# Second-pass products as four 32-column tiles, and a planner that counts mode changes: a four-block graph network on one core

## The chip, the core and the metric

The kernel runs on one core of a Trainium2 chip. The metric is device time in microseconds (us) of one execution. Before the change three executions took 1333.88, 1335.44 and 1337.19 us; the median is 1335.44 us. The profiled execution, from which all durations below come, has a span of 1335.1 us.

## What is computed

The input is `x` of shape (32, 512, 128) and a symmetric 0/1 adjacency `adj` of shape (32, 512, 512), both float32. Four residual blocks follow each other; each begins with a layer norm over the last axis and a ReLU:

```
h = relu(layernorm(x))
x = x + attention(h, adj)      # layer 0: q, k, v = relu(h W + b); softmax over the neighbours of q k^T; times v
h = relu(layernorm(x))
x = x + gcn_lstm(h, adj)       # layer 1: an LSTM of 128 steps over a convolution of the last 128 rows,
                               #          sigmoid((A_norm h) lstm_out)
h = relu(layernorm(x))
x = x + four_layers(h, adj)    # layer 2: four graph layers with skip inputs of width 128, 128, 256, 384
h = relu(layernorm(x))
x = x + prelu(adj (h W) + b)   # layer 3
```

The LSTM of layer 1 couples nothing across the 32 batch elements, but its 128 steps are one chain: each needs the state of the step before.

## The kernel before the change

The function `symmetric` does the work when `adj` is symmetric. (A slower general branch is entered only if a counter found a violation at the end.) It has four kinds of work:

- `pass_1(b)` for each of the 32 batch elements: layer norm, keys and values, attention of the last 128 rows alone, and the convolution that feeds the LSTM (tile `f_seq`).
- `lstm()`: 128 steps. A step is a product on TensorE (line 1200), tanh on ScalarE (lines 1226, 1241), three small operations on VectorE (lines 1233 to 1235), tanh (line 1243), one more product and a 32x32 transpose on VectorE (lines 1247 and 1248). The state of all 32 batch elements is only 32 columns wide, so TensorE is used in four *column tiles*: four products, each with a stationary operand of 128 rows and 32 columns, write four groups of 32 PSUM partitions. The function `products` issues these four.
- `pass_2(b)`: attention of the other 384 rows of an element. Its float32 products are `f_pq` (line 1278, one of 384 columns), `f_s` (line 1287, four of 384 columns) and `f_po` (line 1296, twelve of 129 columns), each with a stationary operand of the full 128 columns. For the elements in `EARLY` (before: 0 to 23) it also does the adjacency product of layer 1 (`f_pg`, eight matmuls of 512 columns in a rounded float32 format, line 1380 in `aggregate`) and sends the result to DRAM.
- `rest(b)`: the remainder of layers 1, 2 and 3. For elements outside `EARLY` it also does the `f_pg` product of layer 1 (line 1386).

In `EARLY`, too, `squares` on ScalarE, `relu_parts` on ScalarE and VectorE and `diagonal` on GpSimd belong to `pass_2`. Four calls of `fold` multiply weights of layer 2 together.

No order is written by hand. Every piece of work is recorded as an `Op` with a duration, a rank and its dependences, and `Plan.run` lays the pieces out in time on the engines (a list scheduler), then issues them in the order of their planned starts. On the chip the order per engine is fixed; an engine whose next instruction is not ready waits. Ranks below `URGENT` (1000) are the LSTM's steps; ranks from 20,000 are `pass_2`, from 30,000 `rest`. Pieces of the second pass and the folds are placed between the steps of the LSTM: an urgent piece's expected start holds back longer pieces (the test with 0.15 us). `LATE` (before: 2) elements have their `pass_2` put at the rank of `rest`. `T_STEP` is the planned duration of the LSTM's four tiles, `T_SWITCH` a fixed addition per step. PSUM has eight banks (the cell tag `mm`); one is spared for the LSTM as long as that runs (`spared`), and a test in `room` keeps the last free bank for work that is nearly due.

A float32 product appears in the profile as two records (two passes over the data), each with a weight load (LDWEIGHTS, engine PEld) and a matmul (MATMUL, engine PE); the LSTM's four tiles thus appear as eight of each. A rounded-float32 matmul appears as one.

Of the kernel before, what the change touches and what calls it, by code (L numbers as in the profile page):

```python
# [514 lines left out]


class Op:
    __slots__ = ("engines", "rank", "no", "deps", "cells", "waits", "ready", "end", "engine", "start", "next", "gap")


class Plan:
# [9 lines left out]
    ACROSS = {"PE": 0.2, "ACT": 0.16, "DVE": 0.18, "POOL": 0.18, "SP": 0.25}  # L531
    WITHIN = {"PE": 0.0, "ACT": 0.13, "DVE": 0.12, "POOL": 0.05, "SP": 0.0}
    SLACK = {"PE": 0.25, "ACT": 0.05, "DVE": 0.05, "POOL": 0.05, "SP": 0.05}

    def lag(self, a, b, urgent):

# [24 lines left out]
        c.real = real  # L561
        return c

    def op(self, engines, rank, reads=(), writes=(), after=(), gap=0.0):

        o = Op()
        o.engines, o.rank, o.no, o.gap = engines, rank, len(self.ops), gap
        deps = set(after)
        cells = []
        for acc, is_write in [(a, False) for a in reads] + [(a, True) for a in writes]:  # L570
            c, part = acc if isinstance(acc, tuple) else (acc, None)
            if c not in cells:
                cells.append(c)
            for key, (ws, rs) in c.parts.items():
                if part is None or key is None or key == part:
                    deps.update(ws)
                    if is_write:
                        deps.update(rs)
            mine = c.parts.setdefault(part, ([], []))
            if is_write:  # L580
                c.parts[part] = ([o], [])
            else:
                mine[1].append(o)
        deps.discard(o)
        o.deps = list(deps)
        o.cells = [c for c in cells if c.pool is not None]
        for c in o.cells:
            c.left += 1
        self.ops.append(o)
        return o  # L590

    def run(self, tc, queues):
# [63 lines left out]
        def room(o):  # L656

            at = 0.0
            need = {}
            for c in o.cells:  # L660
                if c not in seen:
                    if c.tag in self.fifo and self.fifo[c.tag][turn[c.tag] + need.get(c.tag, 0)] is not c:
                        return None
                    need[c.tag] = need.get(c.tag, 0) + 1
            for t, n in need.items():
                if len(slots[t]) < n + (t == self.banks and o.rank >= self.spared and self.left > 0):
                    return None
                if len(slots[t]) == n and t in self.kept and by_rank and o.rank > by_rank[-1].rank + 12:
                    return None
                at = max(at, sorted(slots[t])[n - 1])  # L670
            return at
# [2 lines left out]
            if not o.waits:  # L674
                put(o)
        done, order = 0, []
        by_rank = sorted((o for o in ops if o.rank >= self.URGENT), key=lambda o: -o.rank)
        while done < len(ops):
            best = None
            for e, cands in pools.items():  # L680
                first = None
                held = expected.get(e)
                for rank, no, o in cands:
                    r = room(o)
                    if r is None:
                        continue
                    if r:
                        r += self.HOP
                    s = max(free[e], o.ready[e], r)
                    if len(o.engines) > 1:  # L690
                        mine = s + o.engines[e][0]
                        if any(max(free[x], o.ready[x], r) + o.engines[x][0] < mine - 1e-9 for x in o.engines if x != e):
                            continue
                    if rank < self.URGENT:
                        held = s
                    elif held is not None and s < held < s + o.engines[e][0] - 0.15:
                        continue
                    if first is None or s < first[0] - 1e-9:
                        first = (s, o)
                        if s <= free[e] + 1e-9:  # L700
                            break
                if first is not None and (best is None or first[0] < best[0]):
                    best = (first[0], e, first[1])
            assert best is not None, f"no instruction can start, {done} of {len(ops)}"
            s, e, o = best
            for x in o.engines:
                pools[x].remove((o.rank, o.no, o))
            o.start, o.engine, o.end = s, e, s + o.engines[e][0]
            free[e] = o.end
            if o.rank < self.URGENT:  # L710
                foresee(o)
            for c in o.cells:
                if c not in seen:
                    seen.add(c)
                    slots[c.tag].remove(place(c, s) if c.tag == self.banks else min(slots[c.tag]))
                    if c.tag in self.fifo:
                        turn[c.tag] += 1
                c.left -= 1
                c.free_at = max(c.free_at, o.end)
                if c.left == 0:  # L720
                    slots[c.tag].append(c.free_at)
# [18 lines left out]
def symmetric(ctx, tc, x, adj, weights, cols, rows, lstm_b, prelu_a, out, fail):  # L740
# [16 lines left out]
    L = NT - 1  # L757
    NR = N - P
    MANY = 512 // (4 * B)
    LATE = 2  # L760
    EARLY = range(24)
    FOLDS = (4, 7, 10, 13)
    MOVED = range(2, B - 2)
    TURN = 32
    T_STEP, T_SWITCH = 0.24, 0.1
    assert D == P and N == 512

    BUFS = {"a": 2, "ar": 6, "x": 7, "xn": 5, "y": 5, "gs": 5, "inv": 4, "n0": 4, "n1": 4, "n2": 4, "n3": 4, "low": 3, "hp": 2, "dt": 2, "mm": 8, "st": 4, "mv": 4, "rs": 4, "sh": 4, "dg": 8, "dv": 4,
# [58 lines left out]

    def DMA(rank, kb, fn, r=(), w=(), **k):
        return plan.op({"SP": (max(0.45, t_dma(kb)), fn)}, rank, r, w, gap=2.0, **k)

    def turn_tiles(dst, src):

# [353 lines left out]
    def lstm():  # L1186
# [17 lines left out]
                products(z, k, W_IH, seq[:, k, :])  # L1204

        z = biased(0)
        PE(2_000, MANY * T_STEP, lambda z=z: first(z), [], [z], after=conv_ops)
        coming, c = z, None
        for t in range(T):
            R = t  # L1210
# [9 lines left out]
                    products(coming, k, W_IH, seq[:, t + MANY, :])  # L1220
            if t or coming is not None:
                ahead = 0.0 if coming is None else T_STEP
                PE(R, T_SWITCH + ahead + (T_STEP if t else 0.0), step, [], ([z] if t else []) + ([coming] if coming else []),
                   after=last, gap=-ahead)
            th = new("th", (P, 4, TURN), f"f_th_{t}")
            ACT(R, 0.22, lambda th=th, z=z, k=k: nc.scalar.activation(th.t[:, :3, :], z.t[:, k, :3, :], AF.Tanh), [z], [(th, 0)])
            cn = new("c", (P, TURN), f"f_c_{t}")
# [26 lines left out]
    def pass_2(b):  # L1254
# [29 lines left out]
        es = []  # L1284
        for j in range(NT):
            s = bank(f"f_s_{b}_{j}", (P, NR), whole=False)
            PE(R, t_mm(NR), lambda s=s, j=j: nc.tensor.matmul(s.t, keys.t[:, bass.ts(j, P)], q.t, start=True, stop=True),  # L1287
               [keys, q], [s])
            e = new(f"n{j}" if j < 3 else "y", (P, NR), f"f_e_{b}_{j}")
            ACT(R, t_act(NR), lambda s=s, e=e: nc.scalar.activation(e.t, s.t, AF.Exp), [s], [e])  # L1290
            DVE(R, t_dve(NR), lambda e=e, j=j: nc.vector.tensor_mul(e.t, e.t, rows_of(j)), [(mask, j)], [e])  # L1291
            es.append(e)
        po = bank(f"f_po_{b}", (P, L, P + 1), whole=False)
        for t in range(L):
            for j in range(NT):
                PE(R, t_mm(P), lambda t=t, j=j: nc.tensor.matmul(  # L1296
                    po.t[:, t, :], es[j].t[:, bass.ts(t, P)], v.t[:, j, :], start=(j == 0), stop=(j == NT - 1)),
                    [es[j], v], [po])
# [46 lines left out]
    def sums_of_1(rank, b, xc, ar, rs):  # L1345
# [6 lines left out]
        xp = relu_parts(rank, xs, f"c{b}")  # L1352
        pg = bank(f"f_pg_{b}")
        diagonal(rank, ar, OP.add, b in EARLY)
        first = aggregate(rank, xp, ar, pg, b in EARLY)
        gT = xc if b in EARLY else new("gs", (P, N), f"f_gT_{b}")
        evict(rank, N, lambda: gT.t if b not in EARLY else flat(gT.t), lambda: pg.t, [pg], [gT])
        return gT, first
# [15 lines left out]
            parts.t[:, :, 1, :], xs.t, 0.0, f32(parts.t[:, :, 0, :]), OP.max, OP.subtract), [xs, (parts, 0)], [(parts, 1)])  # L1374
        return parts

    def aggregate(rank, parts, ar, pg, single=False):

        for k, j in ((k, j) for k in range(2) for j in range(NT) if single):
            last = PE(rank, t_r(N), lambda k=k, j=j: nc.tensor.matmul(  # L1380
                pg.t, parts.t[:, j, k, :], ar.t[:, j, :], start=(k == 0 and j == 0), stop=(k == 1 and j == NT - 1)),
                [(parts, k), ar], [pg])
        for k in range(0 if single else 2):
            def fn(k=k):
                for j in range(NT):
                    nc.tensor.matmul(pg.t, parts.t[:, j, k, :], ar.t[:, j, :], start=(k == 0 and j == 0),  # L1386
# [277 lines left out]
```

## Time and profile before

| stage (us from the start) | what runs | length | TensorE busy | VectorE busy | ScalarE busy |
|---|---|---|---|---|---|
| 0 to 183 | first pass | 183 | 173.3 | 155.4 | 109.3 |
| 183 to 528 | the LSTM, second pass beside it | 345 | 328.9 | 286.0 | 232.8 |
| 528 to 1335 | `rest` | 807 | 786.8 | 568.3 | 490.6 |

The stages are cut at the first and the last matmul of the LSTM. "Busy" is the time in which an engine has at least one instruction under way; since matmuls overlap in the pipeline, a busy TensorE may still lose time between two of them, and this shows only in the starts of successive matmuls. Over the whole span TensorE is busy for 97%, VectorE 76%, ScalarE 62%, GpSimd 32%. The program moves 236 MB by DMA, a mean of 177 GB/s.

### The profile page before, as it was taken

What the parts mean: (1) busy time and instruction counts of PE and PEld (TensorE: products, weight loads), DVE (VectorE), ACT (ScalarE), POOL (GpSimd) and SP (SyncE); (2) the same over time, 40 slices, a digit from 0 to 9 for tenths busy, and PEclk for the clock granted to TensorE, in tenths of its full rate; (3) what the DMA queues carried; (4) which work ended last, traced back from release to release, by engine and by line L of the source; (5) the groups of instructions that cost most, each with busy time, mean ns of one, the idle gap of its engine ahead of it and who ended that gap; (6) DMA issues with size and microseconds to landing.
All of it is one profiled execution on the core that took longest, in us unless ns stands there. A gap on an engine that the chain in (4) does not pass through costs nothing. (4 is left out here: it accounts for less than half of the span.)

```text
span 1335.1 us, 26488 instructions
## 1 busy us (share of the span) xinstructions
PE 1289.0 (97%) x8831; PEld 990.6 (74%) x8832; DVE 1009.7 (76%) x3388; ACT 832.7 (62%) x2093; POOL 421.4 (32%) x761
## 2 busy tenths in 40 slices
PE   7999999999999999799999999999999999999996
PEld 6888876666666666578787877778787787777774
DVE  7899878887888887756776767777776788787645
ACT  5566667776776566555666757666676666665433
POOL 4655444332243224412231322313132232232101
PEclk9999999999999999899999999999999999999998
DMA  7888888877577578963676665776777366583211
GB/s 237 278 257 278 288 261 268 261 239 232 181 232 251 165 233 211 200 177 79 134 176 157 163 161 151 157 165 152 158 162 160 89 136 134 142 161 84 48 32 35
DMA packets 302177, 236.46 MB, mean 177 GB/s; under 512 B 138320, under 2 KB 246096, under 8 KB 302032
## 3 DMA queue, kind: packets, MB, share of 16 engines
q1 hardware_dynamic: 285136, 217.90, 58.5%
q0 software_dynamic: 16896, 16.78, 8.3%
q8 instruction: 72, 1.18, 0.4%
q14 instruction: 73, 0.60, 0.1%
HBM read 140.12 MB, written 63.05 MB: 152 GB/s over the span
## 5 line engine op out<-in xcount | busy, mean ns | idle before, releaser
L1386 PE MATMUL f_pa<-f_ar,f_y 128*128 128x512 f32 x1024 | 300.9, 430 | 0.2 <-ACT f_y L1364 0.2
L1386 PEld LDWEIGHTS f_pa<-f_ar,f_y 128*128 128x128 f32 x1024 | 189.9, 189 | 73.8 <-issue 39.7
L1478 PE MATMUL f_py<-f_wf,f_n 128*128 128x128 f32 x1280 | 174.0, 275 | 0.3 <-ACT f_n L1493 0.3
L1478 PEld LDWEIGHTS f_py<-f_wf,f_n 128*128 128x128 f32 x1280 | 164.7, 191 | 8.5 <-ACT f_n L1493 0.8
L1489 PE MATMUL f_pa<-f_n,f_wf 128*128 128x512 f32 x320 | 152.8, 592 | 0.0
L1493 ACT ACTIVATE f_n<-f_pa,f_bcol 128x512 f32<-128x512 f32 x128 | 88.3, 690 | 101.7 <-PE f_pa L1489 101.3
L1330 ACT ACTIVATE f_ar<-f_a 128x512 fp32r<-128x512 f32 x224 | 138.6, 620 | 11.1 <-DMA f_a<-in_adj_dram 9.0
L1446 POOL DMA_DIRECT2D f_das<-f_ar x32 | 27.9, 872 | 346.3 <-ACT f_ar L1330 275.2
L1364 ACT CAST f_y<-f_py 128x512 fp32r<-128x512 f32 x128 | 74.9, 585 | 98.8 <-PE f_py L1478 94.8
L1296 PEld LDWEIGHTS f_po<-f_v,f_e 128*128 128x128 f32 x768 | 99.2, 190 | 23.8 <-issue 9.9
L1485 DVE TENSOR_TENSOR f_pa<-f_pa,f_inv 128x512 f32<-128x512 f32 x128 | 86.8, 692 | 34.9 <-PE f_pa L1386 34.8
L1365 DVE TENSOR_TENSOR f_y<-f_py,f_y 128x512 fp32r<-128x512 f32 x128 | 87.5, 684 | 32.9 <-ACT f_y L1364 32.3
L1296 PE MATMUL f_po<-f_v,f_e 128*128 128x129 f32 x768 | 110.2, 281 | 0.5 <-DVE f_e L1291 0.4
L1287 PE MATMUL f_s<-f_q,f_k 128*128 128x384 f32 x256 | 100.6, 502 | 0.8 <-ACT f_q L1281 0.7
L1200 PE MATMUL f_z<-f_w,f_seq 128*32 128x128 f32 x2040 | 82.2, 278 | 14.2 <-DVE f_seq L1248 8.3
L1489 PEld LDWEIGHTS f_pa<-f_n,f_wf 128*128 128x128 f32 x320 | 57.8, 189 | 45.3 <-issue 38.3
L1200 PEld LDWEIGHTS f_z<-f_w,f_seq 128*32 128x32 f32 x2040 | 48.7, 109 | 53.8 <-DVE f_seq L1248 11.7
L1451 DVE SCALAR_TENSOR_TENSOR f_junk<-f_a,f_aT 128x1024 bf16<-128x1024 f32 x64 | 78.0, 1218 | 2.4 <-DMA f_aT<-f_das 1.4
L1386 PE MATMUL f_pg<-f_ar,f_xp_d 128*128 128x512 f32 x256 | 73.8, 410 | 0.0
L1478 PE MATMUL f_py<-f_wf,f_T_c 128*128 128x128 f32 x448 | 73.0, 275 | 0.7 <-ACT f_py L929 0.7
L1290 ACT ACTIVATE f_e<-f_s 128x384 f32<-128x384 f32 x128 | 61.8, 487 | 16.6 <-PE f_s L1287 15.5
L1063 DVE COPY f_hl_d<-f_n 128x1024 uint16<-128x1024 uint16 x25 | 17.3, 693 | 66.3 <-ACT f_n L1493 66.3
(209 smaller groups left out, 2838.5 us busy)
## 6 DMA issues: line engine op xcount, KB each, us to landing
f_a<-in_adj_dram SPq DMA_DIRECT2D x56, 1024.0 KB
f_das<-f_ar POOLq DMA_DIRECT2D x32, 512.0 KB, 5.7
f_dkq<-f_kh SPq DMA_DIRECT2D x32, 448.0 KB
f_dv<-f_v SPq DMA_DIRECT2D x32, 258.0 KB
f_v<-f_dv SPq DMA_DIRECT2D x32, 258.0 KB
f_x<-in_x_dram SPq DMA_DIRECT2D x32, 256.0 KB
f_al<-in_adj_dram SPq DMA_DIRECT2D x32, 256.0 KB
f_k<-f_dkq SPq DMA_DIRECT2D x32, 256.0 KB
```

Of the source, the lines that this page charges most:

```text
L1200: nc.tensor.matmul(z.t[part, k, :, :], h, w[:, m : m + 4, part], start=False, stop=True, skip_group_check=True)
L1287: PE(R, t_mm(NR), lambda s=s, j=j: nc.tensor.matmul(s.t, keys.t[:, bass.ts(j, P)], q.t, start=True, stop=True), [keys, q], [s])
L1296: PE(R, t_mm(P), lambda t=t, j=j: nc.tensor.matmul(po.t[:, t, :], es[j].t[:, bass.ts(t, P)], v.t[:, j, :], start=(j == 0), stop=(j == NT - ...
L1330: ACT(rank, 0.62, lambda t=t: nc.scalar.activation(ar.t[:, t, :], a.t[:, t, :], AF.Square, accum_out=deg.t[:, t : t + 1]), [a], [(ar, t), ...
L1364: ACT(rank, t_act(N), lambda: nc.scalar.copy(parts.t[:, :, 0, :], src.t), [src], [(parts, 0)])
L1365: DVE(rank, t_dve(N), lambda: nc.vector.tensor_sub(parts.t[:, :, 1, :], src.t, f32(parts.t[:, :, 0, :])), [src, (parts, 0)], [(parts, 1)])
L1386: nc.tensor.matmul(pg.t, parts.t[:, j, k, :], ar.t[:, j, :], start=(k == 0 and j == 0), stop=(k == 1 and j == NT - 1))
L1451: nc.vector.scalar_tensor_tensor(junk, flat(a.t[:, 2 * k : 2 * k + 2, :]), 1.0, flat(aT.t[:, 2 * k : 2 * k + 2, :]), OP.mult, OP.not_equal ...
L1478: nc.tensor.matmul(py.t[:, j, :], nodes[n].t[:, bass.ts(j, P)], wf[:, W_F[i] + c, 0, :], start=False, stop=(c == nch - 1), skip_group_chec ...
L1485: before = DVE(R, t_dve(N), lambda pa=pa: nc.vector.tensor_mul(pa.t, pa.t, inv_row.t), [inv_row], [pa])
L1489: nc.tensor.matmul(pa.t, wf[:, W_F[i] + c, 1, :], nodes[n].t, start=False, stop=(c == nch - 1), skip_group_check=True)
L1493: ACT(R, 0.57, lambda pa=pa, n=n, i=i: nc.scalar.activation(n.t, pa.t, AF.Tanh, bias=bcol[:, i : i + 1]), [pa], [n])
```

## The change

1. `by_columns` issues a 128-column product as four products of 32 columns each, into four groups of 32 PSUM partitions. All products of `pass_2` (`f_pq`, `f_s`, `f_po`) go through it. The products of `f_pg`, of the folds and of `rest` stay whole.
2. Each `Op` is marked `tiled` or not; the planner keeps the mode of TensorE and adds `SWITCH` (0.1 us into the tiled mode, 0.2 us out of it) where the mode changes. The fixed `T_SWITCH` goes; `T_STEP` is 0.22 instead of 0.24.
3. `EARLY` is 20 elements instead of 24, `LATE` 3 instead of 2.
4. `aggregate` no longer issues its eight matmuls one by one in `EARLY`, but in two groups of four.
5. Three tests of the planner: the last-bank test counts the spared bank, the held-back test has 0.2 for 0.15, and the list behind the last-bank test starts at rank 10,000.

```diff
+    SWITCH = (0.2, 0.1)
...
-                if len(slots[t]) < n + (t == self.banks and o.rank >= self.spared and self.left > 0):
-                    return None
-                if len(slots[t]) == n and t in self.kept and by_rank and o.rank > by_rank[-1].rank + 12:
+                spare = n + (t == self.banks and o.rank >= self.spared and self.left > 0)
+                if len(slots[t]) < spare or len(slots[t]) == spare and t in self.kept and by_rank and o.rank > by_rank[-1].rank + 12:
                     return None
...
-        by_rank = sorted((o for o in ops if o.rank >= self.URGENT), key=lambda o: -o.rank)
+        tiled = False
+        by_rank = sorted((o for o in ops if o.rank >= 10_000), key=lambda o: -o.rank)
...
+                    if e == "PE" and o.tiled != tiled and rank >= self.spared:
+                        s = max(s, free[e] + self.SWITCH[o.tiled])
...
-                    elif held is not None and s < held < s + o.engines[e][0] - 0.15:
+                    elif held is not None and s < held < s + o.engines[e][0] - 0.2:
...
+            if e == "PE" and o.tiled != tiled:
+                s = max(s, free[e] + self.SWITCH[o.tiled])
...
+            if e == "PE":
+                tiled = o.tiled
...
-    LATE = 2
-    EARLY = range(24)
+    LATE = 3
+    EARLY = range(20)
...
-    T_STEP, T_SWITCH = 0.24, 0.1
+    T_STEP = 0.22
...
+    def by_columns(out, left, right, start, stop):
+        for c in range(P // TURN):
+            part = bass.ts(c, TURN)
+            nc.tensor.matmul(out[part], left[:, part], right, start=start, stop=stop)
...
-                PE(R, T_SWITCH + ahead + (T_STEP if t else 0.0), step, [], ([z] if t else []) + ([coming] if coming else []),
-                   after=last, gap=-ahead)
+                PE(R, ahead + (T_STEP if t else 0.0), step, [], ([z] if t else []) + ([coming] if coming else []),
+                   after=last, gap=-ahead, tiled=True)
...
-        PE(R, t_mm(NR), lambda: nc.tensor.matmul(pq.t, w[:, W_Q, :], hT.t, start=True, stop=True), [hT], [pq])
+        PE(R, t_mm(NR), lambda: by_columns(pq.t, w[:, W_Q, :], hT.t, True, True), [hT], [pq], tiled=True)
...
-            PE(R, t_mm(NR), lambda s=s, j=j: nc.tensor.matmul(s.t, keys.t[:, bass.ts(j, P)], q.t, start=True, stop=True),
-               [keys, q], [s])
+            PE(R, t_mm(NR), lambda s=s, j=j: by_columns(s.t, keys.t[:, bass.ts(j, P)], q.t, True, True),
+               [keys, q], [s], tiled=True)
...
-                PE(R, t_mm(P), lambda t=t, j=j: nc.tensor.matmul(
-                    po.t[:, t, :], es[j].t[:, bass.ts(t, P)], v.t[:, j, :], start=(j == 0), stop=(j == NT - 1)),
-                    [es[j], v], [po])
+                PE(R, t_mm(P), lambda t=t, j=j: by_columns(
+                    po.t[:, t, :], es[j].t[:, bass.ts(t, P)], v.t[:, j, :], j == 0, j == NT - 1),
+                    [es[j], v], [po], tiled=True)
...
-        first = aggregate(rank, xp, ar, pg, b in EARLY)
+        first = aggregate(rank, xp, ar, pg)
...
-    def aggregate(rank, parts, ar, pg, single=False):
-
-        for k, j in ((k, j) for k in range(2) for j in range(NT) if single):
-            last = PE(rank, t_r(N), lambda k=k, j=j: nc.tensor.matmul(
-                pg.t, parts.t[:, j, k, :], ar.t[:, j, :], start=(k == 0 and j == 0), stop=(k == 1 and j == NT - 1)),
-                [(parts, k), ar], [pg])
-        for k in range(0 if single else 2):
+    def aggregate(rank, parts, ar, pg):
+
+        for k in range(2):
```

More of the change, by code (lines that the diff above doesn't have):

```diff
@@ L517 @@
 class Op:
-    __slots__ = ("engines", "rank", "no", "deps", "cells", "waits", "ready", "end", "engine", "start", "next", "gap")
+    __slots__ = ("engines", "rank", "no", "deps", "cells", "waits", "ready", "end", "engine", "start", "next", "gap", "tiled")
 class Plan:
@@ L562, in fixed, with op @@
         return c
-    def op(self, engines, rank, reads=(), writes=(), after=(), gap=0.0):
+    def op(self, engines, rank, reads=(), writes=(), after=(), gap=0.0, tiled=False):
         o = Op()
         o.engines, o.rank, o.no, o.gap = engines, rank, len(self.ops), gap
+        o.tiled = tiled
         deps = set(after)
@@ L1206, in lstm @@
         z = biased(0)
-        PE(2_000, MANY * T_STEP, lambda z=z: first(z), [], [z], after=conv_ops)
+        PE(2_000, MANY * T_STEP, lambda z=z: first(z), [], [z], after=conv_ops, tiled=True)
         coming, c = z, None
```

## The prediction

> **What bounds the kernel now.** I read the page's shares first, then the stages, then TensorE's timeline inside the LSTM's stage, then the waits there.
>
> ```profile
> PE 1289.0 (97%) x8831; PEld 990.6 (74%) x8832; DVE 1009.7 (76%) x3388; ACT 832.7 (62%) x2093; POOL 421.4 (32%) x761
> ```
>
> TensorE has under 4% idle time; no other engine is near. By stage (length; busy time of PE, PEld, DVE, ACT, POOL; clock; DMA share; GB/s):
>
> ```profile
> 0.00:183.00 183.00, 173.32 (x1276) 149.41 (x1276) 155.38 (x689) 109.30 (x224) 93.19 (x248) 1.00 0.85 268
> 183.00:528.00 345.00, 328.93 (x3319) 228.76 (x3319) 285.96 (x1206) 232.80 (x817) 121.78 (x194) 1.00 0.76 229
> 528.00:1335.00 807.00, 786.76 (x4238) 612.48 (x4237) 568.32 (x1496) 490.59 (x1053) 206.42 (x321) 0.99 0.60 134
> ```
>
> TensorE is the bound of all three. The middle stage is where the change acts. Busy time hides what happens between matmuls, so I read starts (start, duration, operation, records):
>
> ```profile
> 183.18 1.30 PE L1200 MATMUL f_z<-f_w,f_seq 128*32 128x128 f32 x40
> 184.41 2.05 PE L1296 MATMUL f_po<-f_v,f_e 128*128 128x129 f32 x16
> ...
> 304.28 1.72 PE L1296 MATMUL f_po<-f_v,f_e 128*128 128x129 f32 x14
> 305.94 0.65 PE L1200 MATMUL f_z<-f_w,f_seq 128*32 128x128 f32 x16
> 306.51 0.71 PE L1296 MATMUL f_po<-f_v,f_e 128*128 128x129 f32 x4
> 307.06 0.39 PE L982 MATMUL f_pw<-f_w,f_wTs 128*128 128x128 f32 x2
> 307.28 0.39 PE L983 MATMUL f_pw<-f_w,f_wTs 128*128 128x128 f32 x2
> ```
>
> A whole pass of 128 columns takes 0.11 us (307.06 to 307.28 is two). Ten quadruples of tiles take 183.18 to 184.41, 1.23 us; single records show 0.109 us from one quadruple to the next, 0.135 for the first, and 0.202 from the last tile to the first whole matmul, where 0.089 would do. So a quadruple of tiles costs what one whole pass costs, and a change of mode costs extra. The LSTM's 16 records (four quadruples) take 305.94 to 306.51, 0.57, against 4 x 0.109 = 0.436: 0.135 too much. The four passes behind them take 0.55 for 0.44: 0.11 too much. Over all 127 returns of the trace the medians are: into tiles 0.093, first quadruple 0.025, out of tiles 0.113, second whole pass 0.104: **0.335 us for a round trip**, 0.1675 per change.
>
> 127 round trips are 42.5 us. The stage from the first to the last LSTM matmul (344.2 us) is thus: products about 283 (whole ones 0.220 each for 129 columns, 0.645 for 384, 0.227 for a rounded 512, tiles as above), changes 42.5, and some 18 of waiting. The waits of the stage (who waited for whom, total, times, longest) show both directions: tanh waits for TensorE, and TensorE waits for the transposed state:
>
> ```profile
> ACT f_th L1226 <- PE f_z L1200: 35.0, 62, 1.6
> ...
> PEld f_z L1200 <- DVE f_seq L1248: 11.7, 23, 1.3
> ...
> PE f_z L1200 <- DVE f_seq L1248: 8.3, 13, 1.5
> ```
>
> The steps themselves, 128 in 342 us (starts of line 1248), last 2.70 us on average, 2.55 in the median, 2.23 at the fifth percentile: the chain has a little room below TensorE's pace, not much.
>
> [...] 0.335 us for a return trip, and four tiles that start 7 ns apart and share one period of 0.109 us. [...] the 40 tile matmuls and their 40 loads above began within 1.03 us, 13 ns each, [...] a whole float32 load (190 ns) is hidden behind the 0.109 us passes as it is.
>
> **The change part by part.**
>
> *Tiled second-pass products.* 32 f_pq, 128 f_s and 384 f_po products become 544 x 2 passes x 4 tiles = 4352 records where there were 1088: PE's records go from 8831 to some 12,095. By the LSTM's quadruples each pass costs what it did, so the products cost 0. Unknown from both sides: tiles are seen with 128 moving columns alone, not with 384; the pass could expose the 0.025 us that the first quadruple of each run shows (1088 x 0.025 = +27 us), or gain nothing. I take 0, because within the runs every product brings new weights and still has 0.109.
>
> *Mode changes.* I counted them in the order of TensorE's instructions of both built programs. Before: 256 in all, 254 between the first and the last LSTM matmul. After: 108, of which 86 there, 11 earlier, 10 later and one at the border. What remains is the work that stays whole: f_pg and the folds. 148 changes fewer x 0.1675 = **-24.8 us** of TensorE time: -28.1 in the LSTM's stage, +1.8 in the first, +1.7 in the last. It is all on the path as long as TensorE is the bound.
>
> *EARLY 20 for 24.* Four elements' f_pg products, 32 matmuls x 0.227 = 7.3 us, move from the LSTM's stage to `rest`: 0 in sum. With them go four squares (16 x 0.81 us on ACT), relu_parts, the layer-norm application and the diagonal: ACT -20, DVE -8.5 us in the stage. `rest` has to do the latter parts again for these four, beside a TensorE that has 787 of 807 us to itself while DVE has 568: hidden. The squares were done twice and the 256 KB sum was written and read back on SP's queue; both go. SP's other transfers keep their number; in `rest` DMA is at 0.60, so what SP is passed by costs nothing.
>
> *LATE 3 for 2.* The third late element's products stand in the LSTM's stage all the same by the order after (it holds 117 f_s and 348 f_po, against 116 and 348): 0.
>
> *Groups of four in f_pg and the planner's tests.* The order is affected, not the amount. A group is 0.9 us and can sit before a step; bounded by one group's half per f_pg group at worst, 40 x 0.45 = +18, and by 0. I take +3, since the planner holds such pieces back when a step is expected (it is part of the 11 below). Its new cost of a change (0.3 for the round trip) stands near the measured 0.335, where 0.1 stood before, so steps planned should be met more often. No wait is added; what stands behind a step on PE is the next second-pass product.
>
> *The stage.* TensorE's work there: 325.8 - 28.1 - 7.3 + 1.3 (one f_pq, one f_s more) = 292. That is 2.28 us per step, now at the chain's fifth percentile of 2.23. Steps with less TensorE work than this leave it idle: laying the order's work out by step and raising each to at least 2.2 gives 305. VectorE comes to (286 - 8.5) / 316 = 88%, from 83%, so some delays of the chain stay: I add 11 for these and the groups, below the 18 of before. 316 us, where there were 344.2: -28.2. The other stages: +1.8 - 0.6 (one f_s fewer) and +7.3 + 1.7 - 0.6 (one f_pq fewer) = +9.6. **Sum: 1335.1 - 28.2 + 9.6 = 1316.5.** The profiled span agrees with the median of 1335.44 within 0.4, so I forecast 1317.
>
> **The rivals.**
>
> *A (65%)*, the above: 1317, own range 1308 to 1327.
>
> *B (14%), the LSTM's chain takes TensorE's place.* With mean times of its parts instead of the best (tile start to tanh 0.53, to the cell 0.39, cell 0.38, to tanh 0.30, to the product 0.35, to the transpose 0.22, transpose 0.21, to the next tile at least 0.15) a step takes 2.53 even if TensorE is never in its way, 2.6 with a little of it: 127 x 2.6 = 330. 1335.1 - 14 + 9.6 = 1331. For it: DVE at 88%. Against it: the long ones among these times are ACT and DVE held up by work that TensorE delivers late, and medians give 2.33.
>
> *C (13%), the new plan is met.* The stage comes down to the 302 to 305 that order and chain allow: 1304.
>
> *D (8%), tiles cost more than whole products.* Place: the 1088 passes of the second pass. Price: if each shows the first quadruple's 0.025, or the four streams of 384 columns hinder each other by as much, +27 us stand against -18.6: 1343. It decides from 18 ns per pass upward. For it: no tile wider than 128 columns is in the trace, and no run longer than 40 records. Against it: the steady 0.109 there.
>
> *That the switches don't go* is excluded by the order; that they cost nothing, by the starts.
>
> **How the numbers follow.** About 0.3% (4 us) is what can be told from no change here: 1331.4 to 1339.4. Faster: A, C and half of B: 0.86. Same: the other half of B, less its tail: 0.06. Slower: D: 0.08. The range leaves out D and a part of C: 1303 to 1332.
>
> **What would show it.** Right: some 12,095 PE records; f_s in quadruples with 0.322 from one to the next and f_po with 0.110; the LSTM's stage at about 316, steps of 2.48 on average; the last stage 8 us longer. If the stage is near 330 with TensorE waiting for line 1248, it is B. If quadruples of f_s or f_po stand 0.13 or more apart, it is D. I would be wrong altogether if the last stage, bound by TensorE at 97%, grew by much more than the 8 us moved into it.

## The result, and the profile after

The changed kernel takes **1349.26 us** (median of 4 executions, 1348.05 to 1351.38) beside 1334.66 us of the kernel before on the same chip. The ratio is **1.0109, 95% interval 1.0088 to 1.0130**: slower by 1.1%, where 1317 us was forecast. The profiled execution has a span of 1347.5 us, 12.4 above the 1335.1 of before.

Its page (busy time of each engine, then the transfers of instructions; before there were 72 of these with 1.18 MB):

```profile
PE 1279.4 (95%) x12099; PEld 978.4 (73%) x12099; DVE 1010.7 (75%) x3392; ACT 819.6 (61%) x2065; POOL 412.6 (31%) x749
...
q8 instruction: 98, 1.61, 0.5%
```

By stage, columns as before (length; PE, PEld, DVE, ACT, POOL; clock; DMA share; GB/s):

```profile
0.00:184.00 184.00, 174.44 (x1408) 147.82 (x1412) 155.89 (x689) 108.61 (x223) 92.72 (x248) 1.00 0.84 268
184.00:526.00 342.00, 308.47 (x6265) 210.59 (x6253) 269.66 (x1174) 221.06 (x782) 109.12 (x179) 0.99 0.72 223
526.00:1347.00 821.00, 796.49 (x4438) 620.04 (x4438) 585.16 (x1530) 489.94 (x1061) 210.72 (x324) 0.98 0.57 131
```

TensorE is busy for 20 us less in the LSTM's stage and idle for 33 us of it, where it was idle for 16. The stage has shrunk only from 344.2 to 341.5 us. The last stage has grown by 14.4. Those are the two things to explain.

TensorE's timeline inside the stage (start, duration, operation, records):

```profile
303.63 0.65 PE L1218 MATMUL f_z<-f_w,f_seq 128*32 128x128 f32 x16 [0.21 <-DVE f_seq L1266]
304.09 0.62 PE L847 MATMUL f_po<-f_v,f_e 128*32 128x129 f32 x16
304.89 0.87 PE L847 MATMUL f_po<-f_v,f_e 128*32 128x129 f32 x24 [0.18 <-issue]
305.58 0.82 PE L847 MATMUL f_s<-f_q,f_k 128*32 128x384 f32 x8
306.23 0.62 PE L1218 MATMUL f_z<-f_w,f_seq 128*32 128x128 f32 x16
306.66 1.47 PE L847 MATMUL f_s<-f_q,f_k 128*32 128x384 f32 x16
```

Here the change does what it says. Eight `f_s` tiles take 305.58 to 306.23, 0.65 us, as two whole passes of 384 columns did. The LSTM's 16 records stand between them with 0.43 us to the next product (306.23 to 306.66) and no change of mode. Over the whole stage a quadruple of `f_s` starts 0.3225 us after the one before, a quadruple of `f_po` 0.110: the prices of the whole passes.

What ended TensorE's idle time has changed, though. The waits of the stage (who waited for whom: total us, times, longest):

```profile
ACT f_th L1244 <- PE f_z L1218: 52.9, 73, 5.5
...
PEld f_po L847 <- issue: 16.8, 58, 3.0
PE f_z L1218 <- DVE f_seq L1266: 16.4, 21, 2.9
PEld f_z L1218 <- DVE f_seq L1266: 14.6, 25, 1.8
```

TensorE's wait for the transposed state has grown from 20.0 us (11.7 and 8.3, before) to 31.0. And single waits of up to 3.0 us "for issue" have appeared, where the longest of `f_po` before was 0.2. Such a wait is one that no semaphore explains.

### The profile page after: what moved, and what is told of

It is laid out like the page before. It is cut to its first block, busy times and chain, and to the rows that moved or that the text cites. A ratio compares the mean times of both kernels' runs of the same rounds, so it can differ in the third digit from the quotient of the medians.

```text
span 1347.5 us, 33002 instructions
## 1 busy us (share of the span) xinstructions
PE 1279.4 (95%) x12099; PEld 978.4 (73%) x12099; DVE 1010.7 (75%) x3392; ACT 819.6 (61%) x2065; POOL 412.6 (31%) x749
## 5 line engine op out<-in xcount | busy, mean ns | idle before, releaser
L1348 ACT ACTIVATE f_ar<-f_a 128x512 fp32r<-128x512 f32 x208 | 129.0, 622 | 10.9 <-DMA f_a<-in_adj_dram 8.0
L847 PE MATMUL f_po<-f_v,f_e 128*32 128x129 f32 x3072 | 110.2, 276 | 7.3 <-issue 5.5
L847 PEld LDWEIGHTS f_po<-f_v,f_e 128*32 128x32 f32 x3072 | 91.1, 111 | 27.5 <-issue 18.1
L1218 PE MATMUL f_z<-f_w,f_seq 128*32 128x128 f32 x2040 | 85.9, 279 | 24.7 <-DVE f_seq L1266 16.4
L847 PE MATMUL f_s<-f_q,f_k 128*32 128x384 f32 x1024 | 105.1, 491 | 0.9 <-ACT f_n L1507 0.8
L1218 PEld LDWEIGHTS f_z<-f_w,f_seq 128*32 128x32 f32 x2040 | 54.5, 110 | 64.3 <-DVE f_seq L1266 14.6
L1400 PE MATMUL f_pg<-f_ar,f_xp_c 128*128 128x512 f32 x256 | 73.3, 415 | 1.0 <-ACT f_xp_c L1390 0.8
```

The costliest lines, as they stand in the source:

```text
L847: nc.tensor.matmul(out[part], left[:, part], right, start=start, stop=stop)
L1218: nc.tensor.matmul(z.t[part, k, :, :], h, w[:, m : m + 4, part], start=False, stop=True, skip_group_check=True)
L1348: ACT(rank, 0.62, lambda t=t: nc.scalar.activation(ar.t[:, t, :], a.t[:, t, :], AF.Square, accum_out=deg.t[:, t : t + 1]), [a], [(ar, t), ...
```

## A ledger of the LSTM's steps

To compare kernels I cut the stage at the first tile of each step that reads the new state, which gives 126 steps. Three things come from the trace for each step: TensorE's work in it (products by their measured durations, plus 0.118 us into tiles and 0.217 out of them, the first passes' extra included); the chain's own time (the interval, less what the transposed state waited for TensorE beyond the shortest 0.06 us); and the interval itself. If nothing else held, a step would last as long as the longer of the first two. The chain's time is that of each run itself: where TensorE delivers the LSTM's own tiles late, that lengthens the chain too. Sums in us:

| kernel | TensorE's work | chain | longer of the two, per step | measured | above it |
|---|---|---|---|---|---|
| before | 318.8 | 308.1 | 335.8 | 339.8 | 4.0 |
| after | 285.0 | 310.9 | 321.3 | 336.3 | 15.0 |
| before's order, tiles (e1) | 296.0 | 312.0 | 328.6 | 337.2 | 8.6 |
| after's order, whole (e2) | 312.5 | 304.2 | 330.6 | 335.5 | 4.9 |
| e6: before, no addition on GpSimd | 318.8 | 288.1 | 323.4 | 326.5 | 3.1 |
| e5: e1, no addition on GpSimd | 296.0 | 294.7 | 314.1 | 326.1 | 12.0 |
| e12: e6, no masks | 318.8 | 289.7 | 325.6 | 329.5 | 3.9 |
| e11: e5, no masks | 296.0 | 292.6 | 313.6 | 324.0 | 10.4 |
| e15: before, addition on VectorE in place | 318.8 | 295.1 | 324.0 | 327.8 | 3.8 |
| e16: e15 with tiles | 296.0 | 302.4 | 319.4 | 331.4 | 12.0 |

The median step lasts the longer of TensorE's work and 2.2 us, plus some 0.02 in the kernels with whole products and 0.05 to 0.1 in those with tiles. Much of the loss sits in a few long steps. From before to after, 33.8 us of TensorE's work go. Of these 19.3 are lost because the chain is then the longer one in its step (14.5 remain of the third column's difference), 11.0 more because TensorE is held up inside its own work, and 3.5 arrive.

## The experiments

### The parts of the change, one by one

e1 is the kernel before, its order kept, with the second pass's products through `by_columns` and nothing else:

```diff
-PE(R, t_mm(NR), lambda s=s, j=j: nc.tensor.matmul(s.t, keys.t[:, bass.ts(j, P)], q.t, ...
+PE(R, t_mm(NR), lambda s=s, j=j: by_columns(s.t, keys.t[:, bass.ts(j, P)], q.t, True, True),
```

> The kernel before, in its own order and with its own planner figures, but with the second pass's 544 products issued as four column tiles each. Mode changes beside the LSTM fall from 254 to 116 by the order (138 x 0.1675 = 23 us of TensorE time). If the LSTM's chain sets the pace (theory P), the stage stays near 340 us and the time near 1331 to 1336. If the fetch of four times as many TensorE instructions starves the engine (theory F), gaps of 1 to 3 us without a producer appear, as in the changed kernel, and the time is 1330 to 1345. If the new order is what costs (theory O), the stage falls to about 320 and the time to about 1312.

e2 is the kernel after, its order kept, with whole products:

```diff
-        for c in range(P // TURN):
-            part = bass.ts(c, TURN)
-            nc.tensor.matmul(out[part], left[:, part], right, start=start, stop=stop)
+        nc.tensor.matmul(out, left, right, start=start, stop=stop)
```

> The changed kernel with its planner, EARLY and LATE, in the same order, but with each second-pass product issued whole, so that TensorE has its 254 mode changes beside the LSTM again and a quarter of the second pass's instructions. Theory P: the stage is TensorE-bound again near 345, the time about 1350 to 1355, a little over the changed kernel. Theory F: no fetch gaps; the 28 us of mode changes come back and the 9 us of gaps go, so about 1360. Theory O: the order is worse whatever the tiles, so about 1365 to 1375.

e3 is the kernel after with `EARLY = range(24)` and `LATE = 2`; e4 the kernel before with `EARLY = range(20)` and `LATE = 3`; e13 and e14 take one of the two alone.

> The changed kernel with EARLY 24 and LATE 2 as before. TensorE's work beside the LSTM is nearly the same by the order (291 us against 292), the last stage's too. P: no change, 1345 to 1352. F: no change, as many instructions. O, if EARLY and LATE are its cause: 8 to 20 us faster than the changed kernel.

> The kernel before with EARLY 20 and LATE 3, whole products, nothing else. TensorE's work beside the LSTM falls by 8 us and the last stage's rises by 7. P and F: 1334 to 1339. O, if EARLY and LATE are its cause: 1342 to 1355.

> The kernel before with EARLY 20 alone (both together cost 17 us). Theory: EARLY puts the rounded sums of four problems, 4 x 1.82 = 7.3 us, into a last stage in which TensorE is the bound, and LATE leaves TensorE without ready work for some 7 us after the LSTM: the time is 1340 to 1345, the last stage longer by 7 to 9, and the first 10 us after the LSTM as before (1.7 us idle). Rival: one of the two carries nearly all, here 1349 to 1353 or 1333 to 1337.

> The kernel before with LATE 3 alone. Theory: the second passes of three problems instead of two follow the LSTM, their products are the same wherever they run, but the waits behind the LSTM's end grow: 1339 to 1345, with some 7 us more of idle TensorE in the first 10 to 60 us after the LSTM. Rival: as for the other one, 1349 to 1353 or 1333 to 1337.

| kernel | median us (range) | ratio to before, 95% interval | LSTM's stage | what follows it |
|---|---|---|---|---|
| before, in the profile | 1335.1 | – | 344.2 | 807.7 |
| after | 1349.26 (1348.05–1351.38) | 1.0109 [1.0088, 1.0130] | 341.5 | 822.1 |
| e1, tiles alone | 1334.99 (1330.54–1340.07) | 1.0010 [0.9996, 1.0024] | 341.3 | 806.2 |
| e2, after but whole | 1347.5 (1345.79–1351.01) | 1.0113 [1.0092, 1.0133] | 340.7 | 819.5 |
| e3, after with 24 and 2 | 1375.81 (1372.97–1380.65) | 1.0318 [1.0288, 1.0348] | 357.3 | 832.6 |
| e4, before with 20 and 3 | 1351.57 (1350.11–1352.17) | 1.0132 [1.0115, 1.0149] | 344.0 | 822.2 |
| e13, EARLY 20 | 1342.53 (1342.09–1343.33) | 1.0056 [1.0039, 1.0073] | 345.6 | 812.3 |
| e14, LATE 3 | 1352.36 (1349.45–1355.03) | 1.0132 [1.0110, 1.0155] | 348.1 | 817.6 |

Two answers. First, the tiles are worth nothing in either order: e1 is the kernel before within 0.3%, e2 the kernel after. Second, with the planner of before, EARLY and LATE are enough for the slowdown: e4 is as slow as the kernel after, and in its last stage as long. e14 shows that LATE alone suffices there, and e13 that EARLY alone costs 7; they don't add up (7 and 17 give 17 together), because each new list of work gives a new order.

With the planner of after, though, they do the opposite. e3 has the tiles and the EARLY and LATE of e1, but the planner and the groups of four of after, and takes 41 us more than e1; EARLY 20 and LATE 3 bring it down by 26.5 us to the kernel after. So the order by itself moves the time by more than the mode changes could be worth, and how much of after's own slowdown is due to EARLY and LATE, how much to the planner, isn't shown: the planner's new tests and the groups of four were not tried alone, with EARLY and LATE as before.

Of the expectations, e1 met theory P's (and F's wider range, with its gaps), e4 met O's and e14 the rival's. e2 came out below all three ranges. e3 was foreseen by none: O had it 8 to 20 us faster than after. e13's time was as expected, but its last stage grew by 4.6 us and not by 7 to 9.

What LATE does shows in the first 60 us behind the LSTM (before, e14, e4; columns as above):

```profile
527.00:587.00 60.00, 51.40 (x288) 39.08 (x288) 40.22 (x121) 35.22 (x91) 20.28 (x37) 0.91 0.88 202
```

```profile
531.00:591.00 60.00, 46.17 (x244) 34.52 (x244) 33.06 (x105) 28.57 (x72) 15.66 (x26) 0.86 0.62 148
```

```profile
528.00:588.00 60.00, 48.28 (x252) 37.51 (x253) 35.28 (x103) 28.23 (x72) 12.04 (x17) 0.83 0.43 112
```

Before, TensorE runs 288 records there, with LATE 3 only 244 and 252: the stage begins with less work ready. TensorE is idle for 13.8 and 11.7 of these 60 us, where it was idle for 8.6. The mean clock is lower too (0.86 and 0.83 for 0.91): it was granted at one half for 10.2 us of this stretch before, for 17.1 in e14 and 19.7 in e4. Summed over what follows the LSTM, TensorE's time beyond its products is 30.4 us before, 37.7 in e14, 37.1 in e4 and in after; these 7 us hold both, the idle time and the slower clock. In e4, 7.2 us of products have moved there as well. These were no relief to the LSTM's stage (344.0 for 344.2): counted as in the ledger, TensorE's work there is 8 us less, but the longer of the two per step only 1 us less.

### What takes TensorE's place: GpSimd's addition

In the trace of before VectorE's instructions of a step are sometimes seven times as long as usual, always under the same GpSimd instruction, layer 1's identity addition:

```profile
236.18 1.28 POOL L1338 TENSOR_TENSOR f_ar<-f_ar,f_ident 128x512 fp32r<-128x512 f32 x1 [2.82 <-DVE f_e L1291]
```

```profile
236.11 0.19 DVE L1233 SCALAR_TENSOR_TENSOR f_cu<-f_th,f_c 128x32 f32<-128x32 f32 x1
236.22 1.29 DVE L1234 SCALAR_TENSOR_TENSOR f_cv<-f_th 128x32 f32<-128x32 f32 x1
237.54 0.19 DVE L1235 SCALAR_TENSOR_TENSOR f_c<-f_cu,f_cv 128x32 f32<-128x32 f32 x1
```

Line 1234 takes 0.18 us elsewhere, here until GpSimd is done. In the stage of before 23 VectorE instructions are prolonged in this way, by 22.9 us together, 10 of them of the chain (9.1 us); after, 16.7 us. All 23 have two inputs (line 1234 two parts of `f_th`). The transpose, which has one, isn't held:

```profile
339.90 1.29 POOL L1338 TENSOR_TENSOR f_ar<-f_ar,f_ident 128x512 fp32r<-128x512 f32 x1
```

```profile
340.02 0.21 DVE L1248 STREAM_TRANSPOSE f_seq<-f_h 128x32 f32<-128x32 f32 x1
340.16 1.05 DVE L1043 SCALAR_TENSOR_TENSOR f_sh_c<-f_ln,f_rs 128x4 f32<-128x4 f32 x1
```

The price can be read off as well: the short instructions end 0.02 to 0.05 us after the GpSimd instruction, the mask's multiplication (0.55 us alone) 0.41 us after it. The number of inputs doesn't tell every case. In after a TENSOR_SCALAR (line 1050, `f_x` and two columns of scalars) takes 1.25 us under the addition where 0.34 is its median, while two instructions of line 1320, with `f_po`, `f_rinv` and `f_x` as inputs, take 0.31 and 0.34 us under another one, the usual time.

e5 (with tiles) and e6 (without) leave this addition out for EARLY, its place in the plan kept, so that the order stays; layer 1's sums then lack the identity.

```diff
-            POOL(rank, 1.4, on(nc.gpsimd), [], [ar])
+            POOL(rank, 1.4, lambda: None, [], [ar])
```

> The run with tiles alone (before's order), with the identity that GpSimd adds to the adjacency left out for the 24 EARLY elements (the planner keeps its place; nothing is issued there, so layer 1's sums lack that term). In the trace of the run with tiles alone every prolonged VectorE instruction of the LSTM's stage lies under this 1.3 us GpSimd instruction: 23 of them, 23 us in sum. Theory P (the LSTM's chain, held up on VectorE, sets the pace once the mode changes are gone): the stage falls from 341 to about 322 and the time by 15 to 22 us, to 1313 to 1320. Theory T (TensorE still sets the pace, through instruction fetch or slower tiles): the stage stays within 5 us of 341 and the time at 1330 to 1336.

> The kernel before, whole products, with the same GpSimd instruction left out for the 24 EARLY elements. TensorE has 326 us of work and mode changes in the stage of 344. P: little room, the stage falls to 333 to 337 at most, the time by 7 to 11 us, about half of what the same edit gives with tiles. T: as much or as little as with tiles.

e7 (tiles) and e8 (whole) record it for VectorE, so that the planner lays everything out anew:

```diff
-        diagonal(rank, ar, OP.add, b in EARLY)
+        diagonal(rank, ar, OP.add)
```

> The run with tiles alone, with the identity added by VectorE (0.68 us each) instead of GpSimd for the EARLY elements; the planner lays its order out anew. P: VectorE loses 23 us of prolongations and gains 16 us of instructions, which the planner can place off the chain: the stage falls to 325 to 335, the time to 1318 to 1328. T: 1330 to 1338.

> The kernel before with the identity added by VectorE for the EARLY elements, whole products. P: the stage is held by TensorE's 326 us and falls by less than with tiles: 336 to 342, the time 1327 to 1334. T: as with tiles.

| kernel | tiles | whole |
|---|---|---|
| e5, e6: addition left out | 1322.08 (1318.92–1324.22), ratio 0.9894 [0.9874, 0.9914] | 1321.42 (1319.9–1324.96), 0.9901 [0.9882, 0.9920] |
| e7, e8: on VectorE, new plan | 1422.85 (1416.32–1424.42), 1.0643 [1.0612, 1.0675] | 1418.39 (1417.98–1420.17), 1.0625 [1.0607, 1.0642] |

Leaving the addition out gains 13 to 14 us in both, where P had the tiles gain twice as much as the whole products; so the collision is no reason why the tiles gain nothing. e7 and e8, some 90 us above all that was expected, say nothing about it, since the new order spoils the last stage: TensorE's share of one and the same stretch of it, first before, then e7:

```profile
560.00:740.00 180.00, 178.98 (x979) 139.80 (x978) 121.83 (x320) 109.22 (x233) 42.17 (x66) 1.00 0.64 146
```

```profile
560.00:740.00 180.00, 124.19 (x572) 83.80 (x570) 59.32 (x152) 54.88 (x113) 19.34 (x33) 0.84 0.30 73
```

e15 (whole) and e16 (tiles) issue the same instruction to VectorE at the place that the plan has for GpSimd. Nothing is left out:

```diff
-            POOL(rank, 1.4, on(nc.gpsimd), [], [ar])
+            POOL(rank, 1.4, on(nc.vector), [], [ar])
```

> The kernel before with layer 1's identity addition issued to VectorE at the very place at which the plan has it on GpSimd; nothing else of the order moves. Theory (GpSimd's 1.28 us prolongs whatever VectorE instruction it meets, and VectorE does the same addition in some 0.65 us): collisions, worth 14 us when the addition was left out, go, 24 x 0.65 us of VectorE come, of which a third to a half delays a step: 1323 to 1330. Rival (VectorE in its fixed order between the LSTM's steps pays for each addition in full): 1332 to 1338.

> The same with the second pass's products as tiles, in the order of before. By the ledger of steps so far a step lasts as long as the longer of TensorE's work in it and some 2.2 us, and what the tiles save is lost to that floor (6 us), to stalls in fetching instructions (5 to 7), to loads that come late, and to waits between ScalarE and TensorE: within 5 us of the whole one, 1321 to 1332. Rival (the tiles pay once GpSimd is out of the way): faster than the whole one by 8 us or more.

e15 takes **1324.24 us (1323.39 to 1325.47), ratio 0.9918 [0.9901, 0.9935]**: it beats both kernels. e16 takes 1330.29 (1323.53 to 1332.83), 0.9959 [0.9943, 0.9975]: with the collision gone, the tiles cost 6 us, one more than expected. VectorE's group of line 1338 in e15 (shortest, median and longest in ns; 24 of the 40 are new):

```profile
L1338 DVE TENSOR_TENSOR f_ar<-f_ar,f_ident x40: 645/683/694, 179.1 to 1221.8; 128x512 fp32r<-128x512 f32 x40
```

VectorE takes 0.68 us for what took GpSimd 1.30 and VectorE up to as much again. In the ledger the chain falls from 308.1 to 295.1 us and the steps follow by 12.0.

### Would the tiles pay if TensorE had more to do, or VectorE less?

e9 (tiles) and e10 (whole) let TensorE do the identity addition, with one more rounded matmul of 128 columns beside each of the eight; a rounded identity is prepared once, and GpSimd's addition is left out (not shown in this cut):

```diff
-                pg.t, parts.t[:, j, k, :], ar.t[:, j, :], start=..., stop=...
+                nc.tensor.matmul(pg.t[:, bass.ts(j, P)], part, ident_r, start=False, stop=False, ...)
+                nc.tensor.matmul(pg.t, part, ar.t[:, j, :], start=..., stop=...)
```

> The order of before and tiles, as the run without the identity addition on GpSimd, but the sums keep the identity: TensorE adds it, with one more rounded matmul of 128 columns behind each of layer 1's eight (weights the same parts, moving operand a rounded identity; GpSimd's place in the plan stays empty). Estimate for one: between 0.057 us (a quarter of the 512-column one) and 0.112 (the floor that the planner's own costs use), so 8.7 to 17 us for some 19 problems in the stage. My theory (with tiles TensorE has some 26 us of waits for the LSTM's chain in this stage, so work added to it is hidden): stage 329 to 336 us, time 1322 to 1331. Rival (tiles gain nothing whatever TensorE's load is, because a queue in order can't use the gaps): the added work comes on top, stage 338 to 346, time 1331 to 1340.

> The same on the kernel before with its whole products. Without the identity addition its stage had only some 4 us of waits on TensorE, so both theories put the added 8.7 to 17 us on top: stage 335 to 345, time 1328 to 1338. What tells the theories apart is the difference to the tiled one: mine says whole is slower by 6 to 13 us, where it was faster by 0.7 without the added work; the rival says 0 again.

e11 (tiles) and e12 (whole) leave out GpSimd's addition and the multiplication of the second pass's exponentials by the mask, which stay unmasked:

```diff
-            DVE(R, t_dve(NR), lambda e=e, j=j: nc.vector.tensor_mul(e.t, e.t, rows_of(j)), [(mask, j)], [e])
+            DVE(R, t_dve(NR), lambda: None, [(mask, j)], [e])
```

> The order of before and tiles, without the identity addition on GpSimd (layer 1's sums lack the identity) and also without the second pass's multiplication by the mask on VectorE (its exponentials stay unmasked); both keep their places in the plan. VectorE loses about 76 x 0.45 = 34 us in the stage. My theory (in the tiled order VectorE's and ScalarE's work between the LSTM's steps holds the stage, TensorE's 303 us do not): stage 305 to 320 us, time 1298 to 1314. Rival (the bare chain of a step, or the order itself, holds it): stage 325 or more, time 1317 to 1323.

> The same omissions on the kernel before with its whole products and its 254 changes of mode. My theory (TensorE's 326 us of products and changes hold its stage already): stage 324 to 330, time 1313 to 1322, so that the tiled one is faster by 8 to 20 us. Rival: no difference between tiled and whole, as in the pairs so far.

| kernel | tiles | whole |
|---|---|---|
| e9, e10: addition on TensorE | 1344.97 (1341.82–1349.44), 1.0068 [1.0051, 1.0084] | 1345.11 (1342.26–1346.43), 1.0080 [1.0063, 1.0097] |
| e11, e12: no masks | 1325.34 (1317.99–1332.6), 0.9934 [0.9909, 0.9960] | 1321.15 (1318.3–1324.82), 0.9890 [0.9872, 0.9908] |

My theory failed both times. I had taken the wait in the tiled stage for slack that added work would fill, and VectorE for what held it. The added 21 us on TensorE came on top in both: the stage is 351.1 us with tiles and 349.0 whole, from 329 and 330. (The time of e9 lies 5 us above even the rival's range.) An added matmul costs 0.11 us, not the quarter of 0.227, as its pairs in e10 show:

```profile
191.27 0.23 PE L1385 MATMUL f_pg<-f_ident,f_xp_c 128*128 128x128 f32 x1
191.33 0.44 PE L1386 MATMUL f_pg<-f_ar,f_xp_c 128*128 128x512 f32 x1
191.61 0.22 PE L1385 MATMUL f_pg<-f_ident,f_xp_c 128*128 128x128 f32 x1
191.67 0.45 PE L1386 MATMUL f_pg<-f_ar,f_xp_c 128*128 128x512 f32 x1
```

A pair takes 0.34 us (191.27 to 191.61) where the wide one alone takes 0.227: the narrow one is followed after 0.06, but the wide one only after 0.28.

With some 34 us less of VectorE the stage hardly moved, 327.0 and 332.9. So VectorE's amount of work doesn't hold it, and the work that was added to TensorE didn't fill its idle time there.

Part of the reason is in the ledger. Counted in the same way, the longer of the two per step sums to 336 us in e9 and 343 in e10, so that the tiles save 7; but TensorE is held up inside its own work for 12 us in e9 and for 3 in e10, which takes all of it back. And much of the idle time isn't spread over the steps but lies in a few incidents. In e11, ten steps hold 14.2 of the 21.1 us beyond the longer of TensorE's work and 2.2 us; in e12 ten hold 7.6 of 9.7. Two kinds of them can be read off the trace.

*Instructions that come late.* In the trace of after:

```profile
210.27 1.27 PE L847 MATMUL f_po<-f_v,f_e 128*32 128x129 f32 x35
214.26 0.98 PE L847 MATMUL f_po<-f_v,f_e 128*32 128x129 f32 x28 [2.73 <-issue]
```

The same tile, the same operands, nothing to wait for, and 2.73 us of standstill. The instructions come in transfers of 16.4 KB: 98 in after for 24,566 records of TensorE (its sequencer's among them), 72 before for 18,005, so one for some 250. In the LSTM's stage of after four such stops last over 1 us (3.0, 1.27, 1.67 and 2.82 us from record to record, 8.8 in all). They come after 4033, 6849, 8897 and 10,177 records, and between these lie 11, 8 and 5 times 256. At each of them k transfers have ended and 449 records beyond the first 256 k are used, and TensorE goes on 1.3 to 1.5 us after the next transfer has ended. There are two such stops in e1 (2.48 and 1.16), four in e5 (6.5), five in e16 (8.9), three in e11 (4.5) and five in e9 (7.3). The kernels with whole products have none over 0.4 us that no semaphore explains. By an estimate from the spacings above, whole products use 256 records in some 14 us (256 x 0.055, two records in 0.11 us) and tiles in 3.5 (256 x 0.0136, eight records in 0.109 us). In before, the shortest time from the start of a transfer to its use is 7.4 us; in after it is 2.2. Two of the four transfers began only after TensorE had stopped (0.65 and 0.4 us); why so late stays open. After two of these stops (at 349.5 and 393.9) TensorE's clock was also granted at 0.5 for 3.4 us.

I didn't try a tiled product with fewer instructions, so how much of the hold-up (the last column of the ledger, 9 to 15 with tiles and 3 to 5 whole) is due to fetching is only read from the steps in which such a stop falls. These hold some 9 of the 15.0 us in after and 6 of the 12.0 in e5, but only 1.5 of the 8.6 in e1, where the stop of 2.48 us falls among the LSTM's own tiles and so counts as chain. The rest of that column stays open.

*A load that comes late.* Near the end of the stage, in after:

```profile
511.09 0.93 SPq L1410 DMA_DIRECT2D f_a<-in_adj_dram  x1
...
520.40 0.63 ACT L1348 ACTIVATE f_ar<-f_a 128x512 fp32r<-128x512 f32 x1 [3.29 <-DMA f_a<-in_adj_dram]
520.94 0.19 ACT L1348 ACTIVATION_READ_ACCUMULATOR f_ar<-f_a 128x1 f32 x1
521.03 0.23 ACT L1244 ACTIVATE f_th<-f_z 128x96 f32<-128x96 f32 x1
...
522.95 0.43 PE L1218 MATMUL f_z<-f_w,f_seq 128*32 128x128 f32 x8 [2.93 <-DVE f_seq L1266]
```

ScalarE waits for an adjacency of `rest` with the LSTM's tanh behind it, and TensorE, which is done, waits 2.93 us for the state. The step takes 5.22 us where TensorE has 2.11 of work. Nearly every kernel has such a step: 4.40 us before, 7.02 in e14, 6.56 in e11. The 33.8 us less of work that TensorE has in after didn't shorten it: 5.22 us for 4.40.

## Why the prediction was wrong

The mode changes and the tiles were right: 12,099 records for 12,095; 0.3225 and 0.110 us apart for 0.322 and 0.110; TensorE's work by step 285.0 us over 126 steps, where 292 were forecast over all; raised to 2.2 us per step it is 297.4, where 305 were forecast. Rival D (tiles cost more) is excluded by the spacing, though its time of 1343 lay nearest.

Two steps make up the error of 31 us, some 25 and 6 of it; a third was as wrong, and how much of the 31 us is due to it isn't shown.

**"I add 11 for these and the groups, below the 18 of before": mis-sized.** The steps lose 38.9 us beyond the longer of TensorE's work and 2.2, where 11 was forecast; before it was 20.0. So the stage is 341.5 us and not 316. I took delays as a small sum on top of TensorE's work, to be smaller in a better plan. They are delays of the chain in single steps, under GpSimd's addition, behind a late load or a late instruction; as long as TensorE has 2.5 us in a step (318.8 us in 126 steps) it covers most of such a delay, and with 2.3 (285.0) it covers less. Of the saved 33.8 us, 19.3 vanish here. That is rival B's mechanism, the LSTM's chain in TensorE's place, to which I gave 14%, though in single steps and not, as B had it, in all of them; I argued it away with the medians of the chain's parts, where the mean was the right measure. The other 11.0 are hold-ups inside TensorE's work. I read the short run of 40 tiles, whose 80 records began 13 ns apart, as proof that the issue of instructions is no limit; 80 are fewer than the 256 counted for one transfer, and in after TensorE stands still four times for 1.27 to 3.0 us over a transfer that comes late.

**"LATE 3 for 2: 0" and "EARLY 20: 0 in sum": both wrong.** The last stage grew by 14.4 us, not 8. Its products grew as forecast (7.2 in e4), but with LATE 3 TensorE loses 7 us more behind the LSTM, idle or at the slower clock. And the 7.3 us that left the LSTM's stage relieved nothing there, as e4's unchanged 344.0 shows: moving work is neutral only while TensorE is the bound at both ends. I had said that a last stage growing by much more than 8 would show me wrong altogether; it did.

**"I take +3" for the groups of four and the planner's tests: mis-sized.** e3 differs from e1 in the planner and these groups alone and takes 41 us more. With EARLY 20 and LATE 3 the same planner finds a better order (26.5 us less). That this brings the kernel after back to e4's time is luck, and nothing that I foresaw. What in the planner's tests costs e3 its time stays open.

The sum: e4, EARLY and LATE alone with the old planner, ratio 1.0132; in after's order with whole products (e2) 1.0113; with tiles 1.0109. The tiles took part in neither direction.

## What to carry to other kernels

Where an engine with a fixed order shares its steps with a serial chain of nearly the same length, a saving on the engine is worth at most the change of the sum of the longer one per step, with the chain's measured times, not its medians (in after 14.5 of 33.8 us, of which 3.5 arrived); count it step by step from the trace before believing it. Look for what prolongs the chain instead: here one line, an addition moved from GpSimd to VectorE at the same place, gave 0.8%, and the 138 mode changes that e1 saves in the stage nothing. And keep the order when trying a part of a change: the same addition on the same engine cost 94 us more in a new plan (e8 against e15).

## What the runs showed of the hardware

- In before, 23 two-input VectorE instructions that met GpSimd's addition (1.28 us) ended only 0.02 to 0.42 us after it (line 1234 took 1.29 us instead of 0.18); a one-input transpose under the same instruction took its usual 0.21. In after a TENSOR_SCALAR was held too (1.25 us instead of 0.34), and line 1320 was not (0.31 and 0.34 us).
- Column tiles with 384 and 129 moving columns took as long as the whole pass (0.3225 and 0.110 us per quadruple). At 13.6 ns per record TensorE stopped in after four times for 1.27 to 3.0 us, until 1.3 to 1.5 us after a late transfer of its instructions; e1 had two such stops (2.48 and 1.16 us) and e16 five (8.9 in all). Some tiled kernels also scatter more: 9.5 us over 12 executions of e1 and 9.3 over 9 of e16, where the kernel before beside them spans 4.8 over 15 and 4.0 over 12; after itself spans 3.3 over 4.
- A rounded float32 matmul of 128 columns between those of 512 added 0.11 us in e10, half of what one of 512 columns takes (0.227).
